# Two steps of scores, then two of weighted sums: regrouping the attention loop of a graph kernel and splitting its PSUM into double and single banks

## The chip, the cores and the metric

One core of a Trainium2 chip runs the whole program. The metric is the device time of one execution in microseconds (us). The kernel before takes 617.71 us (median of 3 runs, 617.64 to 618.38). Runs of one kernel in the same rounds lie within 0.6% of each other (the widest set, the kernel before in the last rounds: 617.75 to 621.27). All runs are of the fast state; in the profiled ones the granted clock, the share of TensorE's full clock that the profile shows, is 0.994 to 0.998.

## The reference, cut to what matters

Sixteen graphs of 1024 nodes with 64 features pass two layers. Layer 0 is attention whose softmax runs over the query axis, layer 1 multiplies by an adjacency matrix again and again.

```python
Q = x @ Wq.T + bq;  K = x @ Wk.T + bk;  V = x @ Wv.T
score = softmax(Q @ K.T, axis=1)          # over the first node axis
out   = (score @ adj) @ V
x     = layernorm(x + out)
# layer 1: x, adj x, 2 adj(adj x) - x, ... , then one weight matrix, a residual, a layernorm
```

The kernel computes `adj @ x` first (a blocked product of 128x128 by 128x512 matmuls) and calls it U. Two graphs share the 128 partitions, 64 each, so there are 8 pairs. A step is one pair and one block of 128 nodes, 64 steps in all.

## The kernel before

Each step has four parts. Its scores on TensorE go to PSUM (`sc`), the memory for TensorE's results; a single bank is here a tile of 512 fp32 columns, a double bank one of 1024. VectorE (DVE) evicts them negated to the tile `e` and takes their minimum along the way. ScalarE (ACT) makes the exponentials and their sum. TensorE then adds `e` times the scaled rows of U (`us`) to an accumulator (`acc`). Between these, the work that follows the attention of earlier pairs is threaded in: the product with Wv (`po`), the norm, the transposition (`pt`) and four groups per pair of layer-1 weights (`pw`).

```python
ps   = tile_pool("ps", bufs=3, PSUM)       # three double banks, 1024 fp32 columns each
pacc = tile_pool("pacc", bufs=1, PSUM)     # one more, for the accumulator

def scores(n):
    sc = [ps_tile(f"sc{j}") for j in range(2)]            # one double bank for each graph
    for h in range(2):
        for j in range(2):                                 # two row tiles of 64, concurrent
            matmul(sc[j][:, half h], GY[64 rows of j], xT[64 rows of j])
    for j in range(2):                                     # DVE: negate, minimum
        tensor_scalar(E[n][:, j], sc[j], -1.0, op0=mult, op1=min, accum_out=NM[n][:, j])
# exponentials(n, j): ACT;  scaled(n): DVE reciprocal and us;  weighted(n): four matmuls into acc

def weigh(p, c):                                           # pw
    pw = ps_tile("pw"); ...four matmuls, 64 rows, 192 columns...
    # pw's evacuation, three pieces: ACT copies to GY, DVE adds into xT, ACT copies to xs
    scalar.activation(GY, ...); vector.tensor_tensor(xT, ...); scalar.activation(xs, ...)

for n, (p, m) in enumerate(steps):
    scores(n + 2); exponentials(n + 2, 0)
    if p and m > 4: weigh(p - 1, m - 5)
    elif p > 1 and m == 0: weigh(p - 2, 3)
    scaled(n + 1)
    weighted(n)
    if m == 7: take(p)                                     # ACT copies acc out
    exponentials(n + 2, 1)
    if p: m == 0: norm_1(p - 1) (po);  m == 1: norm_2;  m == 4: transposed(p - 1) (pt)
```

The program sets the order by hand (`tc.manual_schedule()`), and in the traces ACT and DVE run their instructions in the order in which it writes them (pw's evacuation, for one: 259.37, 259.76 and 260.27 us in the prediction).

## Time and profile before

| | before |
|---|---|
| span of the profiled run | 616.0 us |
| TensorE (PE) busy | 605.6 us, 98% |
| DVE, ACT busy | 337.1 us, 226.0 us |
| TensorE's own waits, whole kernel | 3.4 us |
| attention, first sum to last | 132.49 to 409.42 us |
| one full pair (8 steps) | 36.05 us |

TensorE is the bound and hardly waits. What can be gained lies between its groups, as the lines in the prediction show: their starts are further apart than their work is long.

### The profile page before, as it was taken

Reading aid. Unit: us, or ns where it says so; the run is one execution under the profiler, and the core shown is the slowest. Engines: PE = TensorE matmul, PEld = TensorE weight load, DVE = VectorE, ACT = ScalarE, POOL = GpSimd, SP = SyncE. Lnnn points to the kernel's source line nnn. Section 1 sums busy time; section 2 is a strip of 40 time slices with the busy share of each in tenths; the row PEclk is TensorE's granted clock in tenths of the full one; section 3 lists DMA queues with packets and bytes.
Section 4 is the critical chain, followed back from the end, with each engine's and each line's share of the span. In section 5 each row is a group of like instructions: output and inputs, shape, how many; then the busy total and the mean of one; then the engine's idle time right before and its main releaser. Section 6 shows DMA issues by size and latency. Waiting matters only on the chain. (4 is left out here: it accounts for less than half of the span.)

```text
span 616.0 us, 5816 instructions
## 1 busy us (share of the span) xinstructions
PE 605.6 (98%) x2270; PEld 264.4 (43%) x2270; DVE 337.1 (55%) x560; ACT 226.0 (37%) x379; POOL 78.4 (13%) x40
## 2 busy tenths in 40 slices
PE   8999999999999999999999999999999999999995
PEld 7544444433334344443434434344444444444442
DVE  1696212067677767677776767735462333224535
ACT  4210110156666666676666667651100000000012
POOL 0000004400030300203030020300000000150372
PEclk9999999999999999999999999999999999999998
DMA  8700000000000000000000000000000000010012
GB/s 302 263 0 1 0 1 36 33 0 1 1 1 0 2 1 1 1 1 1 1 0 2 0 2 1 0 1 0 1 0 1 0 0 0 1 69 0 34 70 102
DMA packets 6763, 14.30 MB, mean 23 GB/s; under 512 B 2000, under 2 KB 2000, under 8 KB 6736
## 3 DMA queue, kind: packets, MB, share of 16 engines
q1 hardware_dynamic: 6416, 13.90, 6.1%
q8 instruction: 18, 0.29, 0.2%
q10 hardware_dynamic: 320, 0.03, 0.0%
q14 instruction: 9, 0.07, 0.0%
HBM read 9.73 MB, written 4.19 MB: 23 GB/s over the span
## 5 line engine op out<-in xcount | busy, mean ns | idle before, releaser
L330 DVE TENSOR_SCALAR_CACHE_REDUCE e<-sc 128x1024 f32<-128x1024 f32 x128 | 151.6, 1222 | 68.1 <-PE sc L323 68.1
L337 ACT ACTIVATE e<-e,nm 128x1024 f32<-128x1024 f32 x128 | 146.2, 1143 | 74.6 <-DVE e L330 74.5
L323 PE MATMUL sc<-xT,GY 64*128 64x512 f32 x512 | 128.1, 615 | 0.5 <-DVE e L330 0.5
L360 PE MATMUL acc<-e,us 128*64 128x512 f32 x512 | 124.0, 605 | 0.3 <-DVE us L348 0.3
L185 POOL TENSOR_TENSOR rstd<-var,expo 128x16 f32<-128x16 f32 x13 | 37.7, 2901 | 421.5 <-DVE var L180 421.5
L323 PEld LDWEIGHTS sc<-xT,GY 64*128 64x128 f32 x512 | 44.6, 186 | 73.5 <-issue 49.9
L525 ACT ACTIVATE sq<-GY 128x1024 f32<-128x1024 f32 (+1 forms) x10 | 8.9, 886 | 159.6 <-DVE GY L300 149.9
L284 PE MATMUL p<-T,S 128*128 128x512 f32 x144 | 62.8, 592 | 0.0
L360 PEld LDWEIGHTS acc<-e,us 128*64 128x64 f32 x512 | 31.0, 136 | 71.0 <-issue 62.9
L284 PEld LDWEIGHTS p<-T,S 128*128 128x128 f32 x144 | 27.4, 190 | 34.4 <-issue 34.4
L302 ACT ACTIVATE U<-p 128x1024 f32<-128x1024 f32 x6 | 6.1, 1024 | 76.3 <-PE p L284 76.3
L396 PEld LDWEIGHTS pw<-raw,xT 64*128 64x128 f32 x256 | 21.8, 187 | 17.3 <-issue 7.3
L444 POOL TENSOR_TENSOR xs<-xs,mu 128x1024 f32<-128x1024 f32 x8 | 15.0, 1901 | 102.8 <-DVE T L253 92.0
L396 PE MATMUL pw<-raw,xT 64*128 64x192 f32 x256 | 27.1, 332 | 0.0
L407 DVE TENSOR_TENSOR xT<-pw,raw 128x256 f32<-128x256 f32 x32 | 13.6, 425 | 21.3 <-ACT GY L406 21.3
L337 ACT ACTIVATION_READ_ACCUMULATOR e<-e,nm 128x1 f32 x128 | 24.0, 188 | 0.0
L110 ACT ACTIVATE xT<-pt 128x1024 f32<-128x1024 f32 x16 | 16.2, 1014 | 17.2 <-PE pt L109 17.2
L284 PE MATMUL acc<-T,aT 128*128 128x512 f32 x48 | 21.4, 594 | 0.0
L284 PE MATMUL p<-GY,aT 128*128 128x512 f32 x48 | 21.3, 596 | 0.0
L284 PE MATMUL p<-T,aT 128*128 128x512 f32 x48 | 21.3, 592 | 0.0
L284 PE MATMUL acc<-T,S 128*128 128x512 f32 x48 | 21.1, 592 | 0.0
L284 PE MATMUL p<-S,aT 128*128 128x512 f32 x48 | 21.1, 592 | 0.0
(116 smaller groups left out, 585.4 us busy)
## 6 DMA issues: line engine op xcount, KB each, us to landing
aT<-in_adjT_dram SPq DMA_DIRECT2D x8, 512.0 KB, 11.3
out_dram<-GY SPq DMA_DIRECT2D x16, 256.0 KB, 2.2
xs<-in_x_dram SPq DMA_DIRECT2D x7, 512.0 KB, 6.4
aT<-in_adjT_dram SPq DMA_DIRECT2D x1, 1024.0 KB, 5.2
xs<-in_x_dram SPq DMA_DIRECT2D x2, 256.0 KB, 3.0
w1s<-in_w_dram SPq DMA_DIRECT2D x2, 80.0 KB, 10.0
wq<-in_wqT_dram ACTq DMA_DIRECT2D x2, 16.0 KB, 3.3
wk<-in_wkT_dram SPq DMA_DIRECT2D x2, 16.0 KB, 3.1
```

The source lines that it names most:

```text
L110: nc.scalar.activation(xT[:, p], pt, AF.Copy)
L185: nc.gpsimd.tensor_tensor(rstd, var, expo[:, 0:g], ALU.pow)
L284: nc.tensor.matmul(pt[:, ts(i, H)], left_of(k, 2 * g + i), right_of(k), start=(start and k == 0), stop=(k == HB - 1), skip_group_check=not ...
L302: nc.scalar.activation(at(res), got, AF.Copy)
L323: nc.tensor.matmul(sc[j][:, ts(h, H)], GY[s, p, ts(m, P)], xT[s, p, ts(h, H)], start=True, stop=True,)
L330: nc.vector.tensor_scalar(E[n][:, j], sc[j], -1.0, None, op0=ALU.mult, op1=ALU.min, accum_out=NM[n][:, j : j + 1],)
L337: nc.scalar.activation(E[n][:, j], E[n][:, j], AF.Exp, bias=NM[n][:, j : j + 1], scale=-1.0, accum_out=SM[n][:, j : j + 1],)
L360: nc.tensor.matmul(ACC[p][j * C : (j + 1) * C, ts(h, H)], us[:, j], es[:, j, ts(h, H)], start=(m == 0), stop=(m == K8 - 1),)
L396: nc.tensor.matmul(pw[:, j, ts(k, 3 * C)], xT[s, p, ts(2 * c + k, P)], raw[s, 0:3].rearrange("p w c -> p (w c)"), start=True, stop=True,)
L407: nc.vector.tensor_tensor(at(xT), to[:, 0], raw[:, 4:5, None].to_broadcast([P, 2, 2, C]), ALU.add)
L444: nc.gpsimd.tensor_tensor(rows_of(p), rows_of(p), mu[:, p, :, None].to_broadcast([P, G, C]), ALU.subtract)
L525: nc.scalar.activation(sq, r, AF.Square)
```

## The change

The intent: the shape in which scores use the array (64x128, two row tiles) differs from that of the sums (128x64, two column tiles). If two steps of scores run together and then two of sums, half of the changes of shape disappear. Two steps of scores at once need four score tiles, so PSUM is divided anew: two double banks and two single banks, and in each step one graph takes the double bank and the other the two single ones. Below, a turn is two steps, and a pair has turns 0 to 3. The diff also moves pw: before, three of a pair's four groups stood behind the scores of the pair's last three steps and the fourth in the next pair; now one group opens each turn, in front of the scores and so in front of their evictions.

```diff
-    ps = tile_pool("ps", bufs=3, PSUM)
+    ps = tile_pool("ps", bufs=2, PSUM)
+    phalf = tile_pool("phalf", bufs=2, PSUM)
...
-        sc = [ps_tile(f"sc{j}") for j in range(2)]
+        jh = n % 2
+        half, full = halves_tile("sh"), ps_tile("sc")
...
         for j in range(2):
+            if j == jh:
+                for h in range(2):
+                    leave_psum(E[n][:, j, ts(h, H)], half[h], nh[:, h : h + 1])
+                nc.vector.tensor_tensor(NM[n][:, j : j + 1], nh[:, 0:1], nh[:, 1:2], ALU.min)
+            else:
+                leave_psum(E[n][:, j], full, NM[n][:, j : j + 1])
...
+    for n in range(0, len(steps), 2):
+        p, m = steps[n]
+        turn = m // 2
+        ahead = n + 2 < len(steps)
+        if turn == 3 and p:
+            weigh(p - 1, 0)
+        elif turn < 3 and p > 1:
+            weigh(p - 2, turn + 1)
+        if ahead:
+            scores(n + 2)
+            exponentials(n + 2, 0)
+            exponentials(n + 2, 1)
+        scaled(n + 1)
+        if turn == 1 and p:
+            norm_3(p - 1)
+        if ahead:
+            scores(n + 3)
+            exponentials(n + 3, 0)
+        if turn == 0 and p:
+            norm_1(p - 1)
+        elif turn == 2 and p:
+            transposed(p - 1)
+        if ahead:
+            exponentials(n + 3, 1)
+        weighted(n)
+        weighted(n + 1)
+        if turn == 3:
+            take(p)
+        if turn == 0 and p:
+            norm_2(p - 1)
+        if ahead:
+            scaled(n + 2)
```

The rest of the diff (cut) moves the first transpositions to the accumulator's bank, puts the p4 product's second half behind the first two steps of scores, lets some products of the later stages use single banks, splits the norm into three functions, and gives `e` four buffers.

More of the change, by code (lines that the diff above doesn't have):

```diff
@@ L47, in gnn_kernel @@
     small = ctx.enter_context(tc.tile_pool(name="small", bufs=4))
-    ps = ctx.enter_context(tc.tile_pool(name="ps", bufs=3, space=bass.MemoryType.PSUM))
+    ps = ctx.enter_context(tc.tile_pool(name="ps", bufs=2, space=bass.MemoryType.PSUM))
+    phalf = ctx.enter_context(tc.tile_pool(name="phalf", bufs=2, space=bass.MemoryType.PSUM))
     pacc = ctx.enter_context(tc.tile_pool(name="pacc", bufs=1, space=bass.MemoryType.PSUM))
@@ L52, in ps_tile, with halves_tile, acc_tile @@
         return ps.tile([P, 2 * H], FP, tag="ps", name=name)
+    def halves_tile(name):
+        return [phalf.tile([P, H], FP, tag="half", name=f"{name}{h}") for h in range(2)]
+    def acc_tile(name):
+        return pacc.tile([P, 2 * H], FP, tag="acc", name=name)
     xs = big.tile([P, NP, K8, P], FP, tag="xs", name="xs")
@@ L103, in gnn_kernel, with transposed @@
     gb = const.tile([P, 1], FP, tag="gb", name="gb")
-    def transposed(p):
-        pt = ps_tile("pt")
+    def transposed(p, new=ps_tile):
+        pt = new("pt")
         for k in range(K8):
@@ L134, in idle_turns @@
     def idle_turns(n):
-        pt = pacc.tile([P, N], FP, tag="acc", name="idle")
+        pt = halves_tile("idle")[0]
         for _ in range(n):
@@ L140, in gnn_kernel @@
     idle_turns(6)
-    transposed(0)
+    transposed(0, acc_tile)
     idle_turns(4)
@@ L145, in gnn_kernel @@
     idle_turns(2)
-    transposed(2)
+    transposed(2, acc_tile)
     score_weight_2(pm)
+    transposed(3)
     for p in range(NP):
-        if p + 3 < NP:
-            transposed(p + 3)
+        if 0 < p < NP - 3:
+            transposed(p + 3, acc_tile)
         project(p)
@@ L204, in gnn_kernel, with quarter_tile @@
     left, right = slice(0, H), slice(H, N)
-    def quarter_tile(tag, name, bufs):
-        return att.tile([P, 2, N], FP, tag=tag, name=name, bufs=bufs).rearrange(
+    def quarter_tile(name):
+        return att.tile([P, 2, N], FP, tag="e", name=name, bufs=4).rearrange(
             "p a n -> p (a n)"
@@ L211, in left_tiles @@
     def left_tiles():
-        return {n: quarter_tile("e", f"S{n}", 3) for n in (2, 4, 1)}
+        return {n: quarter_tile(f"S{n}") for n in (2, 4, 1)}
     def left_sum(S, n):
@@ L226, in by_pair, with product @@
         return t.rearrange("p k (q f) -> p q k f", q=NP)
-    def product(S, src, res, plus=None, acc_group=0):
+    def product(S, src, res, plus=None, acc_group=0, in_halves=()):
         pairs, blocks = (slice(0, NP // 2), slice(NP // 2, NP)), (low, high)
@@ L243, in sums @@
             if n == 1:
-                T[1] = quarter_tile("r", "T", 1)
+                T[1] = quarter_tile("T")
             t = by_pair4(S[1] if n == 3 else T[1])
@@ L277, in step @@
                 if chain == "a" and g == acc_group:
-                    open_[chain, g] = pacc.tile([P, N], FP, tag="acc", name="acc")
+                    open_[chain, g] = acc_tile("acc")
+                elif (chain, g) == ("b", 1) or chain in in_halves:
+                    open_[chain, g] = halves_tile(name)
                 else:
@@ L281, in step, with read @@
             pt = open_[chain, g]
+            split = isinstance(pt, list)
             for i in rows:
+                to = pt[i] if split else pt[:, ts(i, H)]
                 for k in range(HB):
                     nc.tensor.matmul(
-                        pt[:, ts(i, H)], left_of(k, 2 * g + i), right_of(k),
+                        to, left_of(k, 2 * g + i), right_of(k),
                         start=(start and k == 0), stop=(k == HB - 1), skip_group_check=not start,
                     )
-            got = pt.rearrange("p (i q f) -> p q i f", i=2, q=NP // 2)[
-                :, :, rows[0] : rows[-1] + 1
-            ]
+            for part in [(i,) for i in rows] if split else [rows]:
+                read(
+                    pt[part[0]] if split else pt[:, part[0] * H : (part[-1] + 1) * H],
+                    qi, qc, g, part,
+                )
+        def read(pt, qi, qc, g, rows):
+            got = pt.rearrange("p (i q f) -> p q i f", i=len(rows), q=NP // 2)
             b0 = qi * HB + 2 * g + rows[0]
@@ L294, in at @@
                 return t[:, pairs[qc], b0 : b0 + len(rows)]
-            mark = (qi, qc, g, rows[0]) if len(rows) == 1 else (qi, qc, g)
-            known = any(m in seen for m in (mark, mark[:3]))
-            seen.add(mark)
+            known = all((qi, qc, b0 + i) in seen for i in range(len(rows)))
+            seen.update((qi, qc, b0 + i) for i in range(len(rows)))
             if known:
@@ L323, in scores, with leave_psum @@
                 nc.tensor.matmul(
-                    sc[j][:, ts(h, H)], GY[s, p, ts(m, P)], xT[s, p, ts(h, H)],
-                    start=True, stop=True,
+                    half[h] if j == jh else full[:, ts(h, H)],
+                    GY[s, p, ts(m, P)], xT[s, p, ts(h, H)], start=True, stop=True,
                 )
         NM[n] = small.tile([P, 2], FP, tag="nm", name="nm")
-        E[n] = att.tile([P, 2, N], FP, tag="e", name="e", bufs=3)
-        for j in range(2):
-            nc.vector.tensor_scalar(
-                E[n][:, j], sc[j], -1.0, None, op0=ALU.mult, op1=ALU.min,
-                accum_out=NM[n][:, j : j + 1],
-            )
+        nh = small.tile([P, 2], FP, tag="nh", name="nh")
+        E[n] = att.tile([P, 2, N], FP, tag="e", name="e", bufs=4)
+        def leave_psum(to, sc, least):
+            nc.vector.tensor_scalar(
+                to, sc, -1.0, None, op0=ALU.mult, op1=ALU.min, accum_out=least
+            )
+        for j in range(2):
+            if j == jh:
[4 more added lines that the diff above has]
+                leave_psum(E[n][:, j], full, NM[n][:, j : j + 1])
         SM[n] = small.tile([P, 2], FP, tag="es", name="es")
@@ L355, in weighted @@
         if m == 0:
-            ACC[p] = pacc.tile([P, N], FP, tag="acc", name="acc")
+            ACC[p] = acc_tile("acc")
         es, us = E.pop(n), US.pop(n)
@@ L375, in norm_1, with norm_2, norm_3 @@
             nc.tensor.matmul(po[:, ts(k, P)], rT[:, ts(k, P)], wv, start=True, stop=True)
-        both = att.tile([P, 2, N], FP, tag="r", name="r").rearrange("p a (g c) -> p a g c", g=G)
-        r, sq = both[:, 0], both[:, 1]
-        nc.vector.tensor_add(r, po.rearrange("p (g c) -> p g c", g=G), rows_of(p))
-        nc.scalar.activation(sq, r, AF.Square)
-        LN[p] = r, sq
-    def norm_2(p, last=False):
-        r, sq = LN.pop(p)
+        LN[p] = po
+    def norm_2(p):
+        r = rows_of(p)
+        nc.vector.tensor_add(r, LN.pop(p).rearrange("p (g c) -> p g c", g=G), r)
+        LN[p] = att.tile([P, N], FP, tag="rT", name="sq").rearrange("p (g c) -> p g c", g=G)
+        nc.scalar.activation(LN[p], r, AF.Square)
+    def norm_3(p, last=False):
+        r, sq = rows_of(p), LN.pop(p)
         if last:
-            nc.vector.tensor_tensor(rows_of(p), r, inverse_root_2(sq, G), ALU.mult)
+            nc.vector.tensor_tensor(r, r, inverse_root_2(sq, G), ALU.mult)
         else:
             rstd = inverse_root(row_sums(sq))
-            nc.gpsimd.tensor_tensor(rows_of(p), r, rstd, ALU.mult)
+            nc.gpsimd.tensor_tensor(r, r, rstd, ALU.mult)
     def weigh(p, c):
@@ L435, in gnn_kernel @@
     step("p4", 0)
+    step("p4", 1, (0,))
     for i in range(2):
-        step("p4", 1, (i,))
         scores(i)
@@ L440, in gnn_kernel @@
             exponentials(i, j)
+    step("p4", 1, (1,))
     nc.sync.dma_start(aT[:, low, right], a_in[:, low, right])
@@ L446, in gnn_kernel @@
         )
-    last = len(steps) - 1
-    for n, (p, m) in enumerate(steps):
-        if n + 2 <= last:
+    for n in range(0, len(steps), 2):
[7 more added lines that the diff above has]
+        if ahead:
             scores(n + 2)
             exponentials(n + 2, 0)
-        if p and m > 4:
-            weigh(p - 1, m - 5)
-        elif p > 1 and m == 0:
-            weigh(p - 2, 3)
-        if n + 1 <= last:
-            scaled(n + 1)
+            exponentials(n + 2, 1)
[11 more added lines that the diff above has]
+            exponentials(n + 3, 1)
         weighted(n)
-        if m == K8 - 1:
+        weighted(n + 1)
+        if turn == 3:
             take(p)
-        if n + 2 <= last:
-            exponentials(n + 2, 1)
-        if p:
-            if m == 0:
-                norm_1(p - 1)
-            elif m == 1:
-                norm_2(p - 1)
-            elif m == 4:
-                transposed(p - 1)
+        if turn == 0 and p:
+            norm_2(p - 1)
+        if ahead:
+            scaled(n + 2)
     def blocked(t):
@@ L479, in gnn_kernel @@
     S = left_tiles()
-    step, sums = product(S, blocked(GY), by_pair(Z), xs)
-    weigh(p - 1, 3)
+    step, sums = product(S, blocked(GY), by_pair(Z), xs, in_halves=("c",))
+    weigh(p - 1, 1)
     step("p2", 0, (0,))
     norm_1(p)
-    norm_2(p, last=True)
+    norm_2(p)
+    norm_3(p, last=True)
     step("p2", 0, (1,))
+    weigh(p - 1, 2)
     left_sum(S, 1)
-    step("p2", 1)
+    step("p2", 1, (0,))
+    weigh(p - 1, 3)
+    step("p2", 1, (1,))
     transposed(p)
```

## The prediction

> **What bounds the kernel now.** I read the shares of the engines first, then what TensorE (PE) waited for, then the order of instructions in the attention stage (133 to 409 us).
>
> ```profile
> PE 605.6 (98%) x2270; PEld 264.4 (43%) x2270; DVE 337.1 (55%) x560; ACT 226.0 (37%) x379; POOL 78.4 (13%) x40
> ```
>
> PE is busy nearly throughout. Its own waits come to 3.4 us in the whole kernel:
>
> ```profile
> PE pt L109 <- DMA xs<-in_x_dram: 1.5, 1, 1.5
> PE idle L138 <- DVE still L66: 1.1, 1, 1.1
> PE sc L323 <- DVE e L330: 0.5, 1, 0.5
> PE acc L360 <- DVE us L348: 0.3, 1, 0.3
> ```
>
> So data waits are not the cost. But a busy PE can still lose time between groups, and the starts in the timeline show it (start, duration, then the group):
>
> ```profile
> 262.03 1.94 PE L360 MATMUL acc<-e,us 128*64 128x512 f32 x8
> 263.90 2.00 PE L323 MATMUL sc<-xT,GY 64*128 64x512 f32 x8
> 265.72 0.82 PE L396 MATMUL pw<-raw,xT 64*128 64x192 f32 x8
> 266.48 1.94 PE L360 MATMUL acc<-e,us 128*64 128x512 f32 x8
> ...
> 272.78 2.05 PE L375 MATMUL po<-wv,rT 128*128 128x128 f32 x16
> 274.76 1.99 PE L323 MATMUL sc<-xT,GY 64*128 64x512 f32 x8
> 276.68 1.94 PE L360 MATMUL acc<-e,us 128*64 128x512 f32 x8
> 278.55 1.99 PE L323 MATMUL sc<-xT,GY 64*128 64x512 f32 x8
> ```
>
> Durations overlap, so I use start to start. The last weighted sum takes 278.55-276.68 = 1.87 us, scores followed by a weighted sum 276.68-274.76 = 1.92. Both are eight instructions in four concurrent pairs, and a 512-column instruction streams in 0.429 us (the big product's groups of 16 start 6.87 us apart in the chain of waits), so the pure work is 4 x 0.429 = 1.717. Overhead: 0.20 per group of scores, 0.15 per group of sums, 0.35 us per alternation. Scores before pw (layer weights, the same 64-row shape) take 265.72-263.90 = 1.82, which is 0.10 less: leaving a shape costs 0.10, staying in it nothing. Wv (po) takes 1.98, a transposition (pt, at 253.85) 1.02.
>
> **What the Trainium skill says.** "TensorEngine Tiling (Array Packing)", Key Properties: changing the tiling mode drains TensorE, changing only the tile does not. The 1.92 against 1.82 agrees. "TensorE: Matmul & The Clock Gate", Part 3: matmuls start and end strictly in program order. So a group of scores whose bank is not free holds back everything behind it; in this trace that shows once (130.58 us, below). "PSUM — Partial Sum Buffer", PSUM bank collisions: two engines must not touch one bank at once, so it is to be guarded by bank. The trace agrees: the three evacuations of pw run one after another on ACT, DVE, ACT (259.37, 259.76, 260.27 us), although they read different columns. The two single banks of the change are such guarded units too.
>
> **The change part by part.** The loop does steps n+2, n+3 of scores in one run, then the sums of n, n+1.
>
> 1. Switches: one alternation fewer per two steps, 32 x 0.352 = -11.3 us. po and pt stay separate groups with their own switches: 0. Small waits around pt (sc 1.87 against 1.82, pw 0.85 against 0.75), 0.15 in six pairs: -0.9.
>
> 2. Start of the stage. Now scores 1 and 2 together take 132.49-127.27 = 5.22 instead of 3.43+0.20:
>
> ```profile
> 127.27 2.84 PE L323 MATMUL sc<-xT,GY 64*128 64x512 f32 x10
> 130.58 1.98 PE L323 MATMUL sc<-xT,GY 64*128 64x512 f32 x6 [0.47 <-DVE e L330]
> 132.49 1.94 PE L360 MATMUL acc<-e,us 128*64 128x512 f32 x8
> ```
>
> The changed order puts a 3.5 us product after scores 0 and 1, in which DVE catches up: -1.6, and one switch -0.3.
>
> 3. End of the stage. Two more pw groups move from the loop, where they switch nothing, between 128x128 products: about +0.3 each, +0.6.
>
> 4. PSUM. The score buffers go from three double banks to two double banks plus two single banks. Step n+3 wants both single banks that step n+2 has just filled. DVE must empty them first, so from here the order on DVE and ACT matters:
>
> ```profile
> 252.09 1.22 DVE L330 TENSOR_SCALAR_CACHE_REDUCE e<-sc 128x1024 f32<-128x1024 f32 x1 [1.00 <-PE sc L323]
> 253.24 0.08 DVE L330 DVE_READ_ACCUMULATOR e<-sc 128x1 f32 x1
> 253.24 1.22 DVE L330 TENSOR_SCALAR_CACHE_REDUCE e<-sc 128x1024 f32<-128x1024 f32 x1
> 253.41 1.15 ACT L337 ACTIVATE e<-e,nm 128x1024 f32<-128x1024 f32 x1 [1.41 <-DVE e L330]
> ```
>
> An eviction of 1024 columns occupies DVE for 1.145 us; it starts 0.20 after its scores have streamed; its exponential starts 0.10 after the accumulator is read and holds ACT for 1.14. Estimates from this: a 512-column eviction 0.62 (reductions of 512 and 1024 columns differ by 0.52), its bank free 0.72 after it starts, the extra minimum 0.25. The reciprocal and us take 0.49.
>
> One turn (two steps) with pw, PE in us from its start: pw to 0.75, scores n+2 to 2.465, n+3 to 4.18, drained 4.28, two sums to 7.87. DVE gets the second half of n+2 at 2.665 and then has 0.62+0.25+1.145 (n+2), 0.49, 1.145+0.62+0.62+0.25 (n+3) = 5.14, so it ends at 7.80. The last exponential runs to 9.04: 1.2 us into the next turn. In front of the next evictions the program puts pw's: ACT 0.37, then DVE 0.42, and only then may DVE read the first half, 0.72 to release. That series follows the late exponential.
>
> - Turns 1 and 3 begin with ACT nearly free: scores n+3 are 0.08 late.
> - Turn 0: the late exponential (9.04) is followed by the 1.02 us copy of the accumulator, so ACT is free at 2.20. GY to 2.57, DVE add to 3.02, first half free at 3.74, where PE wanted it at 2.465: 1.27 late. po then needs the double bank of n+2, read at 5.74 instead of 5.56: 0.18. Sum 1.45.
> - Turn 2: norm_3 has put a reduction (1.21) and a small operation (0.2 with gaps) ahead of n+3's evictions in turn 1. DVE ends at 9.23, ACT at 10.47, which is 2.53 into turn 2. GY 2.90, add 3.36, half free 4.08: 1.61 late, and pt 0.17. Sum 1.78.
>
> Per pair with everything in it (2 to 7): 1.45+0.08+1.78+0.08 = +3.4 against 1.41+0.15 saved. Pair 1 has pw only in turn 3: 0.06, po 0.4, 0.06, 0.9 after the norm, 0.08, so +1.5. Pair 0: 4 x 0.06 = +0.2. New waits: 6 x 3.4 + 1.5 + 0.2 = +22.1.
>
> DVE's sum is not over the budget: a full pair gives it 8 x 2.9 + 1.7 (four adds) + 2.6 (norm) = 27.5 us of PE's 34.5. It is order, not load.
>
> Sum: 617.7 - 11.3 - 0.9 - 1.9 + 0.6 + 22.1 = 626.3 us.
>
> **The rivals.**
>
> A. Only the switches count: without part 4, 617.7-13.5 = 604.2. For it: PE waits 0.8 us on DVE in the whole kernel today, DVE has 20% to spare, and the order looks chosen with care. Against it: today a third double bank gives slack and pw's evacuation stands behind the scores' on DVE, whereas the change puts it in front. With 0.08 us per turn it would be 606.7.
>
> B. Only one of the two late turns bites. Without turn 0's, 6 x 1.45 less, 617.6; without turn 2's, 6 x 1.78 less, 615.6. For it: POOL, ACT and DVE hand-overs are each worth some hundredths, and my order of them may be wrong in one. Against it: each lateness is above 1.2 us, made of measured durations.
>
> C. DVE becomes the bound, the half evictions and the minimum costing more than 0.62 and 0.25. Each 0.1 on every half and minimum adds 0.6 per turn to DVE, 2.4 per pair. Then turns 1 and 3 would be late as well and the time goes to 635 or more. Against it: fixed costs are small, 1.145 us for 1024 columns.
>
> **Range and chances.** I trust the lateness in general at about three to one. Weighting 626.3 by 0.75 and 613 (between A and B) by 0.25 gives 623.0. The range 605 to 631 takes in both ends. Faster by 2% means under 605.4, which needs A nearly whole: 0.15. Slower by 2% means above 630.1, part 4 too small or C: 0.08. Within 2%: 0.77.
>
> **What would show it.** Right: between two groups of scores no gap; groups of sums 3.58 us from start to start; new PE waits on the evictions (sc on e) of some 20 us in all, 1.2 to 1.7 us each in turns 0 and 2, with ACT's GY copy starting over 2 us after the turn began; PE busy well below 98%. Wrong: the same turn 7.9 us long in every place (A), or sums waiting on us (C). Wrong above all if ACT does pw's first copy within a microsecond of pw's end in turns 0 and 2.

## The result, and the profile after

The changed kernel took 623.41 us (median of 4 runs, 622.89 to 624.61), the kernel before 618.05 in the same rounds. The ratio is 1.0087, 95% interval 1.0066 to 1.0107. Ratios here are the mean time of one kernel's fast runs over that of the other's in the same rounds, so they are not quite the ratio of the medians quoted.

The engines' line of the page, after:

```profile
PE 603.4 (97%) x2270; PEld 281.0 (45%) x2270; DVE 351.1 (57%) x757; ACT 230.1 (37%) x380; POOL 78.4 (13%) x40
```

TensorE's share fell by one point only, although the span is 5.4 us longer. TensorE's own waits, after (total, times, longest):

```profile
PE sc L341 <- ACT xs L439: 6.8, 12, 0.8
...
PE p L297 <- ACT xs L439: 0.7, 1, 0.7
```

Twelve waits of scores for ACT's copy of pw to `xs`, the last piece of pw's evacuation, are new: two in each of the six pairs 2 to 7. A wait counts here only from the modelled end of the matmul before, so starts say more. TensorE in turn 2 of pair 3, after:

```profile
285.82 0.92 PE L425 MATMUL pw<-raw,xT 64*128 64x192 f32 x8
...
287.87 0.59 PE L341 MATMUL sh<-xT,GY 64*128 64x512 f32 x1
287.87 0.59 PE L341 MATMUL sc<-xT,GY 64*128 64x512 f32 x1
289.24 0.69 PE L341 MATMUL sc<-xT,GY 64*128 64x512 f32 x1 [0.78 <-ACT xs L439]
289.43 0.69 PE L341 MATMUL sh<-xT,GY 64*128 64x512 f32 x1
...
291.47 1.06 PE L117 MATMUL pt<-ident,xs 128*128 128x128 f32 x8
292.46 3.65 PE L387 MATMUL acc<-e,us 128*64 128x512 f32 x16
296.04 0.92 PE L425 MATMUL pw<-raw,xT 64*128 64x192 f32 x8
```

The two sums take 296.04-292.46 = 3.58 us, where two single ones took 2 x 1.87 = 3.73: the saved switch is there. But the scores of n+3, due 0.43 us after 287.87, start at 289.24, which is 0.94 late. `sh` is the single bank, `sc` the double one. ACT and DVE in the same turn, after:

```profile
286.80 1.15 ACT L364 ACTIVATE e<-e,nm 128x1024 f32<-128x1024 f32 x1 [0.18 <-DVE nm L358]
...
287.95 0.36 ACT L435 ACTIVATE GY<-pw 128x256 f32<-128x256 f32 x1
288.34 0.42 DVE L436 TENSOR_TENSOR xT<-pw,raw 128x256 f32<-128x256 f32 x1 [1.18 <-ACT GY L435]
288.69 0.68 DVE L350 TENSOR_SCALAR_CACHE_REDUCE e<-sh 128x512 f32<-128x512 f32 x1
288.80 0.38 ACT L439 ACTIVATE xs<-pw 128x256 f32<-128x256 f32 x1 [0.49 <-DVE xT L436]
```

ACT is still busy with the last exponential of the turn before (286.80), and pw's first copy starts 2.13 us after the turn began. DVE idles 1.18 us for it, adds, and only then reads the first half. Both things that scores n+3 need come out of this series: pw's double bank at 289.18 (end of the copy to xs) and the single bank at 289.37 (its accumulator read).

The turns from start to start, in us. "Bare" is the work with its switches and no waits, from the prediction's pieces (7.86, plus po 1.98 or pt 1.02):

| full pair | turn 0 | turn 1 | turn 2 | turn 3 | sum |
|---|---|---|---|---|---|
| bare | 9.84 | 7.86 | 8.88 | 7.86 | 34.44 |
| predicted | 11.29 | 7.94 | 10.66 | 7.94 | 37.83 |
| after | 10.70 | 8.06 | 10.22 | 8.06 | 37.04 |
| before | | | | | 36.05 |

Where the 5.4 us come from, by stretches of the two traces: loading and products -0.3; start of the stage up to the end of pair 0 -2.0; pair 1 -1.0 (two pw groups fewer); pairs 2 to 6 five times +0.99; pair 7 +0.5; from there to the product p5, the first of layer 1 that multiplies sums of blocks, +2.9 (those two pw groups 2.1, and a wait of 0.7 on a double bank); the rest +0.3.

Turns 1 and 3 hold a smaller loss of 0.20 us, the same in pair 0, where no pw is near (7.41 instead of 7.22). TensorE in turn 3, after:

```profile
298.09 0.59 PE L341 MATMUL sh<-xT,GY 64*128 64x512 f32 x1
298.09 1.01 PE L341 MATMUL sc<-xT,GY 64*128 64x512 f32 x2
298.61 0.69 PE L341 MATMUL sh<-xT,GY 64*128 64x512 f32 x1
298.94 0.59 PE L341 MATMUL sc<-xT,GY 64*128 64x512 f32 x1
299.14 0.59 PE L341 MATMUL sh<-xT,GY 64*128 64x512 f32 x1
```

In step the two row tiles start together every 0.43 us. The first `sh` of n+3 waits for its single bank and starts at 298.61 instead of 298.52, and its successor follows after 0.53 (299.14), not 0.43. From there on the two tiles run staggered, and the block ends 0.19 late: 0.09 of wait and 0.10 of restart. The 0.53 is not special to a held-up tile: when scores begin behind sums, both tiles take 0.54 and 0.53 from their first start to the second (`sh` 136.31 and 136.85, `sc` 136.32 and 136.85).

### The profile page after: what moved, and what is told of

It is laid out like the page before. It is cut to its first block, busy times and chain, and to the rows that moved or that the text cites. A ratio compares the mean times of both kernels' runs of the same rounds, so it can differ in the third digit from the quotient of the medians.

```text
span 621.4 us, 5989 instructions
## 1 busy us (share of the span) xinstructions
PE 603.4 (97%) x2270; PEld 281.0 (45%) x2270; DVE 351.1 (57%) x757; ACT 230.1 (37%) x380; POOL 78.4 (13%) x40
## 4 chain that ended last, share of the span: by engine, by line
PE 75%; DVE 16%; ACT 5%; DMA 1%; issue 1%; SPq 0%; ACTq 0%; DVEq 0%
PE p L297 31%; PE acc L297 13%; PE acc L387 11%; DVE e L350 10%; PE sh L341 7%; PE sc L341 3%; PE pw L425 3%; PE po L402 3%; ACT e L364 2%; PE pg L139 2%; PE pt L117 2%; DVE var L188 1%; DMA xs<-in_x_dram 1%; DVE xT L436 1%; ACT rT L396 1%; DVE nm L358 1%
## 5 line engine op out<-in xcount | busy, mean ns | idle before, releaser
L341 PE MATMUL sc<-xT,GY 64*128 64x512 f32 x256 | 118.8, 597 | 6.8 <-ACT xs L439 6.8
L341 PE MATMUL sh<-xT,GY 64*128 64x512 f32 x256 | 122.9, 605 | 0.1
L387 PE MATMUL acc<-e,us 128*64 128x512 f32 x512 | 116.9, 598 | 0.0
L350 DVE TENSOR_SCALAR_CACHE_REDUCE e<-sh 128x512 f32<-128x512 f32 x128 | 84.7, 687 | 22.4 <-PE sc L341 22.4
L350 DVE TENSOR_SCALAR_CACHE_REDUCE e<-sc 128x1024 f32<-128x1024 f32 x64 | 77.8, 1218 | 0.0
L387 PEld LDWEIGHTS acc<-e,us 128*64 128x64 f32 x512 | 33.9, 136 | 70.0 <-issue 67.1
L341 PEld LDWEIGHTS sh<-xT,GY 64*128 64x128 f32 x256 | 42.5, 186 | 22.6 <-issue 14.9
L319 ACT ACTIVATE U<-p 128x1024 f32<-128x1024 f32 (+1 forms) x7 | 6.3, 902 | 76.1 <-PE p L297 76.1
L425 PEld LDWEIGHTS pw<-raw,xT 64*128 64x128 f32 x256 | 20.1, 186 | 24.1 <-issue 24.1
L425 PE MATMUL pw<-raw,xT 64*128 64x192 f32 x256 | 28.9, 347 | 0.0
L321 DVE TENSOR_TENSOR GY<-p,xT 128x1024 f32<-128x1024 f32 (+1 forms) x9 | 8.9, 986 | 22.4 <-PE p L297 22.4
```

What stands on the lines that cost most here:

```text
L341: nc.tensor.matmul(half[h] if j == jh else full[:, ts(h, H)], GY[s, p, ts(m, P)], xT[s, p, ts(h, H)], start=True, stop=True,)
L350: nc.vector.tensor_scalar(to, sc, -1.0, None, op0=ALU.mult, op1=ALU.min, accum_out=least)
L387: nc.tensor.matmul(ACC[p][j * C : (j + 1) * C, ts(h, H)], us[:, j], es[:, j, ts(h, H)], start=(m == 0), stop=(m == K8 - 1),)
L425: nc.tensor.matmul(pw[:, j, ts(k, 3 * C)], xT[s, p, ts(2 * c + k, P)], raw[s, 0:3].rearrange("p w c -> p (w c)"), start=True, stop=True,)
```

## The experiments

The theory: order and not load. ACT and DVE reach pw's evacuation late in turns 0 and 2, because the accumulator's copy (turn 0) and norm_3's reduction (through late evictions, turn 2) stand in front of it, and the lateness goes to TensorE through the buffers. Rival 1: two double banks are too few, whatever the order. Rival 2: DVE has too much to do. All ten kernels gave correct results.

### e1_copy_later

```diff
+        if turn == 0 and p:
+            take(p - 1)          # behind weigh's evacuation, next turn
         if ahead:
             scores(n + 2)
...
-        if turn == 3:
+        if turn == 3 and not ahead:
             take(p)
```

> The changed kernel, with the accumulator's copy (take) put behind the evacuation of pw at the start of turn 0, instead of in front of it. Theory (order: ACT is late at the start of turn 0 and so pw's double bank and the first single bank come free late): pw's first copy starts about 0.7 us earlier in turn 0, scores n+3 there lose their 0.6 us of lateness, po then waits some 0.25 us for the double bank of n+2, so turn 0 goes from 10.70 to about 10.28 us in six pairs: 621 us, against 623.4 of the changed kernel. Rival 1 (scarcity: two double banks are too few for pw and two steps of scores, whatever the order): turn 0 stays at 10.7, no change. Rival 2 (load: DVE has too much to do): no change either, DVE's work is the same.

Measured: 621.82 us (ratio to before 1.0056, 1.0041 to 1.0071). Turn 0 went from 10.70 to 10.39, the other turns stayed. ACT at the start of turn 0 (which begins at 267.13) in this run:

```profile
268.10 0.38 ACT L435 ACTIVATE GY<-pw 128x256 f32<-128x256 f32 x1
268.97 0.38 ACT L439 ACTIVATE xs<-pw 128x256 f32<-128x256 f32 x1 [0.49 <-DVE xT L436]
269.25 1.02 ACT L396 ACTIVATE rT<-acc 128x1024 f32<-128x1024 f32 x1
```

pw's copy starts 0.97 us into the turn, instead of 268.76-267.07 = 1.69. The lateness of scores n+3 is gone, but po now waits for the double bank of step n+2, whose release the lateness had hidden: 0.36 us, more than the 0.25 that I expected. Half of the gain was given back at the next buffer. For turn 0 order is confirmed; rival 1 holds for this remainder.

### e2_norm_early

```diff
+        if turn == 1 and p:
+            norm_3(p - 1)        # at the start of the turn
         if turn == 3 and p:
             weigh(p - 1, 0)
...
-        if turn == 1 and p:
-            norm_3(p - 1)
```

> The changed kernel, with norm_3 (a reduction and a small operation on DVE, then GpSimd) put at the very start of turn 1, where DVE idles until pw is ready, instead of in front of the evictions of n+3. Theory: turn 1's last exponential ends 1.4 us earlier, so in turn 2 pw's first copy starts within 1 us of pw's end, the 1.04 us lateness of scores n+3 goes, pt waits some 0.25 us: turn 2 from 10.22 to about 9.3 us in six pairs, pair 1 also some 0.6: about 617.5 us. Rival 1 (scarcity): turn 2 stays at 10.2. Rival 2 (load): DVE's work is the same, no change.

Measured: 622.77 us (1.0081, 1.0057 to 1.0106). Turn 2 fell only to 9.91, and turn 1 of pair 1 grew from 7.60 to 8.16. A third of the gain came, and in pairs 2 to 7 turn 1 grew by 0.05 to 0.12 besides. The next run's trace shows what took the rest.

### e3_both

> Both edits of order at once. Theory: they act in different turns, so they add up: a pair 35.7 us (before 36.05, changed 37.04), the kernel about 615.3 us, 0.4% under the kernel before. If they overlap (one lateness only moves to the other turn), the sum is less than the two gains: 617 or more. Rivals 1 and 2: 623.

Measured: 620.15 us (1.0028, 1.0017 to 1.0040). A pair takes 36.42 us. The gains in turn 0 and turn 2 add up (37.04-0.31-0.31), so they act in different turns, but 5 us of the expected gain are missing. Turn 1 of pair 3 in this run, GpSimd and DVE:

```profile
280.76 1.90 POOL L417 TENSOR_TENSOR xs<-xs,rstd 128x1024 f32<-128x1024 f32 x1
...
281.50 1.32 DVE L375 TENSOR_TENSOR us<-U,ri 128x128 f32<-128x128 f32 x1
...
282.73 1.21 DVE L350 TENSOR_SCALAR_CACHE_REDUCE e<-sc 128x1024 f32<-128x1024 f32 x1
```

us takes 1.32 us, where all 64 of them took 0.29 in the kernel before and in the changed one. Its end, 282.82, follows on the end of GpSimd's product of norm_3 at 282.66. My edit had moved that product onto it. In pair 1 the two began almost together, and us took 1.98:

```profile
172.55 1.90 POOL L417 TENSOR_TENSOR xs<-xs,rstd 128x1024 f32<-128x1024 f32 x1
...
172.63 1.98 DVE L375 TENSOR_TENSOR us<-U,ri 128x128 f32<-128x128 f32 x1
```

All seven such us of this run, and all seven of e2 (1.38 to 1.98 us), end 0.15 us after the product. The Trainium skill, "SBUF — State Buffer", Who interferes with whom, says that a DVE instruction with two SBUF inputs contends with a GpSimd instruction that reads SBUF. This run agrees for the product (SBUF is the memory that holds the other tiles): us was slowed, and the eviction beside it, which reads PSUM, was not (from 280.16, 1.22 us). It does not for every GpSimd instruction. The power that norm_3 takes before the product also reads SBUF, and in the kernel before us ran beside it seven times, at 0.29 us each:

```profile
280.98 2.90 POOL L185 TENSOR_TENSOR rstd<-var,expo 128x16 f32<-128x16 f32 x1 [31.17 <-DVE var L180]
...
283.29 0.29 DVE L348 TENSOR_TENSOR us<-U,ri 128x128 f32<-128x128 f32 x1
```

So in e3 the evictions of n+3 again began 1.0 us late.

### e4_both_gap

As e3, with a matmul of 64 columns put on one row tile between the two steps of scores.

```diff
+        if jh and n > 1:
+            s = slice(0, C)
+            nc.tensor.matmul(full[:, 0:64], GY[s, p, ts(m, P)], xT[s, p, 0:64], start=True, stop=True)
```

> As e3, with one extra small matmul (64 rows, 64 columns, about 0.11 us, its result is overwritten) between the scores of n+2 and n+3. In the changed kernel each turn has 0.19 us between them: the single bank comes free 0.09 us late, and the second row tile, once held up, runs staggered and loses another 0.10. If that is a wait of 0.09 with a cost of its own, the extra work hides it: the scores' block of a turn goes from 3.73 to 3.64 us although TensorE does more, 31 x 0.09 = 2.8 us less, 612.5 us. Rival: the 0.19 is no wait (a cost of changing banks between steps); then the extra work is added: 31 x 0.1 = 3 us more than e3.

Measured: 620.52 us (1.0039, 1.0026 to 1.0053). A turn of pair 0 takes 7.44 instead of 7.41. Neither expectation holds. The filler ran on the row tile of the double bank, but the late tile is the one of the single bank: in the timeline its first matmul again comes 0.09 late (260.75 after 260.23+0.43), and the next again 0.53 later. I had filled the wrong tile. A filler on both tiles was not run. So the 0.09 of wait and 0.10 of restart are read from starts, and no run took them away.

### e5_us_early

As e3, and the reciprocal and us of n+1 at the start of each turn, where DVE has nothing to do.

```diff
         ahead = n + 2 < len(steps)
+        scaled(n + 1)
...
-        scaled(n + 1)
```

> As e3, and the reciprocal and us of n+1 moved to the very start of each turn. In e3 one us per pair took 1.3 to 1.98 us instead of 0.29, while GpSimd did norm_3's product of 1.90 us, and this gave back the gain of turn 2 (9.91 instead of the 9.3 expected). Theory (collision of two instructions that both read SBUF on DVE and GpSimd): with us out of the stretch 4.1 to 6.0 us of turn 1 no us takes over 0.3 us, turn 2 goes to about 9.35, pair 1's turn 1 from 8.16 to 7.6: about 616 us (span 614.3). Rival (turn 2 is late because two double banks are too few): us may be short again, but turn 2 stays near 9.9, 619.5 us or more.

Measured: 616.05 us (0.9968, 0.9956 to 0.9981), faster than both kernels, though by 0.3% only against the kernel before. No us takes over 0.294 us. Turn 2 takes 9.43 (292.31-282.88), turn 1 of pair 1 7.41, a full pair 35.93. TensorE at the start of turns 2 and 3 of pair 3, and its own waits on DVE in the stage, this run:

```profile
282.88 0.92 PE L425 MATMUL pw<-raw,xT 64*128 64x192 f32 x8
...
292.31 0.92 PE L425 MATMUL pw<-raw,xT 64*128 64x192 f32 x8
```

```profile
PE pt L117 <- DVE e L350: 2.1, 7, 0.3
PE po L402 <- DVE e L350: 2.1, 7, 0.3
```

No score waits for ACT any more. The theory is confirmed with the collision as its missing part. The edit does two things, though: it ends the collision, and it takes us out from in front of the evictions of n+3. The trace of e3 tells them apart. In turn 3 of pair 3 us stands at the same place (4.81 us into the turn, 4.82 in turn 1) but without a product beside it: it takes 0.29, the evictions of n+3 start 5.02 us into the turn instead of 6.05, and pw's first copy in the next turn comes after 0.97 us instead of 1.81. So the collision alone is enough to make that turn late. DVE is busier than in the changed kernel (355.9 against 351.1 us) and the kernel 7 us faster, which rules out rival 2.

### e6_extra_late

```diff
         if turn == 3:
             take(p)
+            if 0 < p < NP - 1:
+                nc.scalar.activation(LN[p], LN[p], AF.Copy)
```

> The changed kernel with one suspected cost doubled: right behind the accumulator's copy at the end of turn 3 ACT copies the same tile onto itself once more (about 0.9 us), in six pairs. Theory (ACT's lateness at the start of turn 0 is handed on to TensorE nearly one to one): turn 0 from 10.70 to about 11.6 us, 6 x 0.9 = 5.4 us more, 628.8 us, though ACT is busy only 37% of the time. Rivals (scarcity of banks, load of DVE): ACT has room, no change, 623.4.

Measured: 630.36 us (1.0199, 1.0183 to 1.0214). ACT and then TensorE at turn 0 (which begins at 269.78) in this run:

```profile
271.61 1.06 ACT L509 ACTIVATE rT<-rT 128x1024 f32<-128x1024 f32 x1
```

```profile
273.87 0.69 PE L341 MATMUL sc<-xT,GY 64*128 64x512 f32 x1 [1.45 <-ACT xs L439]
```

Turn 0 takes 11.79 instead of 10.70. An ACT copy of 1.06 us costs 1.09 us on TensorE, six times (6.5 of the 7.1 us by which the span grew), though ACT is busy only 38% of the time.

### e7_extra_idle

```diff
         elif turn < 3 and p > 1:
             weigh(p - 2, turn + 1)
+        if turn == 0 and p > 1:
+            nc.scalar.activation(LN[p - 1], LN[p - 1], AF.Copy)
```

> The same extra copy on ACT, but behind pw's evacuation in turn 0, in front of the exponentials, where ACT idles 1.1 us. Theory (place counts, not load): turn 0 stays within 0.1 us of 10.70, 623.5 us. Rival (any more work on ACT in this turn is paid): the same as in e6.

Measured: 623.51 us (1.0089, 1.0075 to 1.0103), turn 0 10.76. The copy on ACT and the first late matmul of n+3 in this run's turn 0:

```profile
269.69 1.05 ACT L489 ACTIVATE rT<-rT 128x1024 f32<-128x1024 f32 x1
```

```profile
269.85 0.69 PE L341 MATMUL sc<-xT,GY 64*128 64x512 f32 x1 [0.36 <-ACT xs L439]
```

The wait is the 0.36 of the changed kernel. The same copy behind pw's evacuation costs 0.06; there it fits the 1.09 us in which ACT idled. Together with e6 this is the cleanest proof: it is the place in ACT's order that is paid for, not the amount of work.

### e8_order_tail

As e5, with one regrouping at the end of the stage.

```diff
     weigh(p, 2)
+    step("p1", 1, (0,))
     weigh(p, 3)
     sums(1)
-    step("p1", 1)
+    step("p1", 1, (1,))
```

> As e5, and at the end of the attention the last layer-weight group is put into the middle of the product p1 g=1 instead of in front of it, where TensorE waited 0.71 us for a double bank. Expected 0.5 us less than e5 (0.8 less wait, 0.2 to 0.3 for one more switch of shape): about 615.5 us, faster than both kernels by some 0.4% and 1.3%.

Measured: 616.44 us (0.9973, 0.9961 to 0.9984). The wait of 0.71 is gone from the list of waits, and the stretch from the last pt to the product p5 shrank from 18.78 to 18.41 us. But the median is 0.4 above e5's in the same rounds, and in the profiled run the first sum begins at 133.37 instead of 132.76, before anything that the edit touches. The local gain of 0.4 is seen in the trace; in the time it is inconclusive.

### e9_pt_between and e10_both_between

On e5, pt between the two sums of turn 2 (e9), and po between those of turn 0 as well (e10).

```diff
-        elif turn == 2 and p:
-            transposed(p - 1)
...
         weighted(n)
+        if turn == 2 and p:
+            transposed(p - 1)
         weighted(n + 1)
```

> As e5, with the transposition pt moved from between scores and sums to between the two sums of turn 2. What is left in e5 over the bare work is 0.19 us per turn (single bank) and 0.36 us of po and pt waiting for the double bank of n+2. If that wait is for the bank alone, the first sum covers it and one more pair of switches costs 0.15: turn 2 from 9.43 to about 9.25 us, seven pairs, 1.3 us less than e5. xT's copy then comes behind the last exponential and may hold up pw of turn 3 by up to 0.1. Rival (the 0.36 is a cost of that switch of shapes): turn 2 gets 0.15 longer, 1 us more.

> As e9, and po too between the two sums of turn 0. Turn 0 itself from 10.39 to about 10.2 us. But po ends 1.8 us later, so the addition, the square on ACT and with them norm_3 at the start of turn 1 come some 0.6 to 1 us later there and push pw's addition and the first eviction back: turn 1 0.4 to 0.7 us longer. Sum: 1 to 3 us slower than e9. If turn 1 stays at 8.06, my account of that chain is wrong.

Measured: e9 617.57 us (0.9980, 0.9971 to 0.9989), e10 620.60 us (1.0026, 1.0013 to 1.0038); the kernel before took 618.82 in these rounds. In e9 pt starts right behind the first sum (291.35-289.48 = 1.87 us, the length of a sum with its switch), so the wait was for the bank. But turn 2 takes 9.50, not 9.25: the next turn's pw now starts 0.27 late, as it waits for xT's copy (`PE pw L425 <- ACT xT L118`, seven times 0.2), which comes last on ACT. A wait was exchanged for another, and instead of the expected 1.3 us less than e5 the run was no faster. In e10 turn 0 fell to 10.19 and turn 1 grew by 0.56 to 8.62, both within what I expected.

## Why the prediction was right or wrong, point by point

The time was predicted as 623.0 and came as 623.41, within 2% as the likeliest class said. The mechanism, gain on switches eaten by new waits, was right. The closeness is partly luck: the sum of the parts was 626.3, and the weighting with 613, a value between rivals A and B, took 3.3 off.

1. **Switches, -11.3.** Right: two sums take 3.58 instead of 3.73 us. A turn of pair 0 takes 7.41 instead of 7.57, which is the 0.35 less the 0.19 of the single bank.
2. **Start, -1.9.** Right: scores 0 and 1 take 3.82, scores 2 and 3 3.83 us, each 3.63 and the single bank's 0.19; the wait of 1.6 is gone.
3. **End, +0.6.** Missed a term: on top of the moved pw groups, a product waits 0.7 for the double bank that pw still holds.
4. **PSUM, +22.1.** The right waits in the right turns, but too large a sum. Turn 0 lost 0.86 (predicted 1.45), turn 2 1.34 (1.78), turns 1 and 3 0.20 each (0.08). All pairs sum to some 18.3: five times 2.6, 2.4 in pair 7, 1.9 in pair 1, 1.0 in the first score blocks. Three sizes were off. The minimum with its reading costs DVE 0.19, not 0.25. The accumulator's copy holds ACT 0.90, not 1.02. And the turns before are longer by the larger 0.19, which gives ACT more time: pw's first copy starts 1.69 into turn 0, not 2.20, and 2.13 into turn 2, not 2.53. Besides, po and pt were to wait 0.18 and 0.17; in pairs 2 to 7 TensorE's list shows no such wait, the late scores hid it.
5. **0.08 in every turn** was the wait alone. That a row tile held up by 0.09 loses another 0.10 was not in the argument.

The sum of the terms as they came out (the first two still reckoned from the trace before), -11.3-0.9-1.9+0.6+0.7+18.3 = +5.5, agrees with the spans' 621.4-616.0 = 5.4.

Of the rivals, A (switches alone) was wrong by 19 us, and C (DVE as the bound) is ruled out by e5. B (only one late turn) did not happen. Of the signs, "between two groups of scores no gap" failed: in turn 2 n+3 came 0.94 late behind n+2. Read as it stands, it also contradicts the prediction's own part 4, which has n+3 1.61 late there. The new waits were to show as some 20 us on the evictions; the profile lists 6.8 us of waits of scores, all on ACT's copy to xs, which let the double bank go 0.19 us ahead of the single one (289.18 and 289.37). That pw's first copy would start over 2 us into the turn held in turn 2 alone. That TensorE's busy share would be "well below 98%" failed: it is 97%, since the modelled matmul durations cover part of each gap.

With the order mended (e5), 1.7 us of span (616.0-614.3) is left of the 14.1 us that points 1 and 2 gain. The rest is in the single bank (32 blocks of scores, 0.19 each, 6.1), in po and pt waiting for a double bank (14 times 0.36, 5.0) and in point 3 (1.3). This is where rival 1 is right: with this division of PSUM no order tried did away with these waits without a new one (e9, e10). Both kernels take eight banks in all. Whether a better use of the eight exists stays open, and so does what the place of pw in front of the scores costs: no run moved it.

## What to carry to other kernels

Grouping instructions to save switches of shape lengthens what must be held in PSUM meanwhile, so before counting the switches saved, lay out one round of every engine and look for the buffer that comes free last. An engine that is busy a third of the time can still be the cause: here, what stood in front of a buffer's evacuation was paid one to one (1.09 us for a copy of 1.06), and the same work behind it, where the engine idled, was nearly free (0.06). When an instruction is moved to an idle place, look at what it sets off on other engines and when: moving a reduction 5 us earlier put a GpSimd product onto a DVE product, and that took back two thirds of the gain.

## What the Trainium skill lacked or had wrong

- "TensorEngine Tiling (Array Packing)", Key Properties, says that a change of tiling mode drains TensorE but gives no cost. Here an alternation of 64x128 and 128x64 costs 0.35 us beyond the work: 0.20 per group of scores, 0.15 per group of sums.
- No page says what happens when one of two concurrent row tiles has to wait for its bank: a start 0.09 us late cost 0.19, as its next matmul came 0.53 instead of 0.43 us later and the tiles then ran staggered.
- "SBUF — State Buffer", Who interferes with whom, says that a DVE instruction with two SBUF inputs contends with a GpSimd instruction that reads SBUF, and makes no difference among these. Here us took 1.31 to 1.98 us instead of 0.29 beside a product of 128x1024 (1.90 us), but 0.29 beside a power of 128x16 (2.90 us), seven times in seven. The profile's spans on GpSimd are rough, and no run shows when the power reads.
